# A six-layer attention stack with a selective scan: the end of the last group but one is given out behind the gates of the last feed-forward, and the ends' rows of x use the first norms' buffers

## The chip, the cores and the metric

The kernel runs on one core of a Trainium2 chip. The metric is the device time of one execution in microseconds (us), lower is better. A core has five engines with a queue each: PE (matrix products and transposes), DVE (vector work), ACT (functions by table, copies out of PSUM), POOL (general element-wise work) and SP, which only issues DMAs here. Each engine works through its own instructions in order, and semaphores join them.

## The reference

The input x has 16 sequences of 256 tokens with 128 features. It is normalised once; the normalised x goes into two branches, and the result is x plus the product of the two.

```python
xn = layernorm(x)
s = selective_scan_branch(xn)        # conv, silu, 16 states, output projection
g = silu(transformer(xn))            # 6 layers, below
return x + s * g

# transformer
for i in range(6):
    x = attn_layer(shift_tokens(x), Wqkv[i], ...) + x     # 16 heads of 64, windows of 32 with look-back
    x = ffn_layer(shift_tokens(x), ...) + x

def ffn_layer(x, g, bln, W1, b1, W2, b2):
    xn = (x - mean) / sqrt(var + 1e-05) * g + bln
    a, gate = split(xn @ W1 + b1)                         # 341 columns each
    return a * gelu(gate) @ W2 + b2
```

`shift_tokens` takes half of the features from the token before. For this case it only means that the kernel writes the two halves of the features with an offset of one token.

## The kernel before

The state x of the transformer stays in SBUF through all layers, transposed (`xT`, features by tokens). The attention works on blocks of 128 tokens: 32 blocks in a layer, 192 in all. The feed-forward works on groups of 512 tokens, two sequences, so eight groups in a layer, numbered 0 to 7. The scan branch runs beside the layers and has put its result `s_of[g]` for each group in DRAM long before the end.

The order of all instructions is written out by hand: the scheduler of the framework is off, and every engine gets its instructions in the order in which the Python code issues them. The main loop runs over n, the number of the block; each turn goes through a fixed list of steps (`order`), each of them for a block some turns ahead or behind. Three of the entries in it are `feed`. A `feed` moves the feed-forward that is at the head of the list `feeds` on to its next `yield`. One feed-forward is put on the list every four turns, as soon as the attention of its group is done.

The stages of `feed_forward` between its yields are, for a group g: the transposes out of `xT` (L336) and the copy `xt` (L340); the statistics (L162, L163, and L167 to L179 on POOL); the norm on ACT (L181); the transposes back (L189) and the copy with gain and bias (L348); the first matrix (L359), the gelu (L367) and the gates (L370); and the second matrix (L382) with the residual sum into `xT` (L385). In the last layer the last stage also puts g on the list `ending`.

`end(g)` writes one group of the result. It loads the rows of x (`xr`, L400) and the scan's result (`sT`, L402), takes the silu of the transformer's state (L405), multiplies it by `sT` (L407), transposes the product (L411), adds the rows of x (L412) and stores `out` (L413). At most one end is given out in each turn, after all steps of the turn. So the end of group g stands behind the whole last stage of the feed-forward of g, and ahead of what the next turn gives out.

The last feed-forward, that of group 7, is put on the list in the last turn, and runs alone after the loop: `feed` is called until it is done, then the last end is given out. The end of group 6 is given out at the end of the last turn, before it.

Tiles of a pool that have the same tag share buffers in turn. Three matter here:

- `xt`, one buffer: the feed-forward's `xt` and the end's `xr`.
- `gl`, two buffers: the three gelu results of a feed-forward and then `sT`.
- `first`, two buffers: the rows of x for the first norms, used only at the beginning (groups 0 to 7).

The feed-forward takes PSUM bank 7 (`f`) for L336, L189 and L382, so L336 of a group has to wait until the residual sum L385 of the group before has read the bank; the end takes bank 1 (`n`) for L411.

Of the kernel before, what the change touches and what calls it, by code (L numbers as in the profile page):

```python
# [8 lines left out]
FP = mybir.dt.float32  # L9
# [6 lines left out]
B, L, DM = 16, 256, 128  # L16
# [8 lines left out]
NG = NT // G  # L25
# [5 lines left out]
def tile_kernel(ctx: ExitStack, tc: tile.TileContext, a, out):  # L31
# [6 lines left out]
    ff = ctx.enter_context(tc.tile_pool(name="ff", bufs=1))  # L38
# [8 lines left out]
    def pair(name):  # L47
        i = int(where[name])
        return psum[:, i : i + 2, :].rearrange("p b x -> p (b x)")

    def bank(name):
        return psum[:, int(where[name]), :]
# [72 lines left out]
    def make_constants():  # L125
        nc.vector.tensor_tensor(twice, mp[:, 2:3], mp[:, 2:3], ALU.add)
        nc.vector.tensor_copy(ident_h, ident)
        nc.vector.tensor_copy(mask, mask_f)
        nc.vector.tensor_tensor(
            w_conv, taps, w_in.unsqueeze(1).to_broadcast([128, 4, 2 * DM]), ALU.mult  # L130
        )
# [7 lines left out]
    def load_ffn_weights(layer):  # L139
        w1 = wts.tile([128, 2 * DI], FP, name="w1")  # L140
        nc.sync.dma_start(out=w1, in_=a["W1"][layer])
        w2 = wts.tile([128, 3, DM], FP, name="w2")
        for c, (c0, n) in enumerate(CH):
            nc.sync.dma_start(out=w2[0:n, c, :], in_=a["W2"][layer, c0 : c0 + n, :])
        ffw_of[layer] = w1, w2
# [25 lines left out]
    def row_stats(pool, xt):  # L171
        mv = pool.tile([128, 4, 2], FP, name="mv", bufs=2)
        bn_rows(pool, mv, xt, range(4))
        return mv, row_rstd(pool, mv)

    def normed(pool, to, xt, mv, rstd):
        less = pool.tile([128, 4], FP, name="less", bufs=2)
        nc.gpsimd.tensor_tensor(less, mv[:, :, 0], rstd, ALU.mult)
        nc.gpsimd.tensor_scalar(less, less, -1.0, None, ALU.mult)  # L179
        for i in range(4):  # L180
            nc.scalar.activation(  # L181
                to[:, i, :], xt[:, i, :], AF.Identity,
                bias=less[:, i : i + 1], scale=rstd[:, i : i + 1],
            )

    def turned(xt, name):
        pt = bank(name)
        for i in range(4):
            nc.tensor.transpose(pt[:, i * 128 : (i + 1) * 128], xt[:, i, :], ident)  # L189
        return pt  # L190
# [3 lines left out]
    def first_norm(g):  # L194

        if len(first_rows) <= g:
            first_rows.append(load_first(g))
        xt = first_rows[g]
        yield
        stats = row_stats(ff, xt)  # L200
        yield
        normed(ff, xt, xt, *stats)
        yield
        pt = turned(xt, "n")
        xn_of[g] = far.tile([128, G], FP, name="xn", bufs=NG)
        for hh, o in halves:
            at = xT[hh, 2 * g : 2 * g + 2, o : o + L]
            nc.scalar.copy(at, pt[hh].rearrange("p (s t) -> p s t", s=2))
            nc.sync.dma_start(out=xn_of[g][hh].rearrange("p (s t) -> p s t", s=2), in_=at)
        yield  # L210
# [116 lines left out]
    def feed_forward(layer, g):  # L327
        if g == 0:
            load_ffn_weights(layer)
        w1, w2 = ffw_of[layer]  # L330
        yield
        yield
        pt = bank("f")
        for i in range(4):
            c0 = (i % NB) * 128
            nc.tensor.transpose(  # L336
                pt[:, i * 128 : (i + 1) * 128], xT[:, 2 * g + i // NB, c0 : c0 + 128], ident
            )
        xt = ff.tile([128, 4, DM], FP, name="xt")
        nc.scalar.copy(xt.rearrange("p n d -> p (n d)"), pt)  # L340
        stats = row_stats(ff, xt)
        yield
        normed(ff, xt, xt, *stats)
        yield
        yield
        pt = turned(xt, "f")
        xn = ff.tile([128, G], FP, name="xn")
        nc.scalar.activation(  # L348
            xn, pt, AF.Identity,
            bias=lnp[:, 1, layer : layer + 1], scale=lnp[:, 0, layer : layer + 1],  # L350
        )
        yield
        yield
        yield
        u = ff.tile([128, 3, G], FP, name="u")
        for c, (c0, n) in enumerate(CH):
            ph = pair(f"h{c}")
            for i in range(2):
                nc.tensor.matmul(  # L359
                    ph[0:n, i * G : (i + 1) * G],  # L360
                    w1[:, i * DI + c0 : i * DI + c0 + n],
                    xn,
                    start=True,
                    stop=True,
                )
            gl = ff.tile([128, G], FP, name="gl", bufs=2)
            nc.scalar.activation(  # L367
                gl[0:n], ph[0:n, G : 2 * G], AF.Gelu, bias=b1[0:n, layer, 3 + c : 4 + c]
            )
            nc.vector.scalar_tensor_tensor(  # L370
                u[0:n, c, :],
                ph[0:n, 0:G],
                b1[0:n, layer, c : c + 1],
                gl[0:n],
                ALU.add,
                ALU.mult,
            )
        yield
        yield
        po = bank("f")  # L380
        for c, (c0, n) in enumerate(CH):
            nc.tensor.matmul(po, w2[0:n, c, :], u[0:n, c, :], start=(c == 0), stop=(c == 2))  # L382
        for hh, o in halves:
            res = xT[hh, 2 * g : 2 * g + 2, o : o + L]
            nc.vector.scalar_tensor_tensor(  # L385
                res,
                po[hh].rearrange("p (s t) -> p s t", s=2),
                b2[hh, layer : layer + 1],
                res,
                ALU.add,  # L390
                ALU.add,
            )
        if layer == DEPTH - 1:
            ending.append(g)
        yield


    def end(g):
        xr = ff.tile([128, 4, DM], FP, name="xr", tag="xt")
        nc.sync.dma_start(out=xr, in_=x_rows[:, 4 * g : 4 * g + 4, :])  # L400
        sT = ff.tile([128, G], FP, name="sT", tag="gl", bufs=2)
        nc.sync.dma_start(out=sT, in_=s_of[g])  # L402
        sg = ff.tile([128, 2, L], FP, name="xn")
        for hh, o in halves:
            nc.scalar.activation(sg[hh], xT[hh, 2 * g : 2 * g + 2, o : o + L], AF.Silu)  # L405
        sg = sg.rearrange("p s t -> p (s t)")
        nc.vector.tensor_tensor(sg, sg, sT, ALU.mult)  # L407
        pt = bank("n")
        for i in range(4):
            cc = slice(i * 128, (i + 1) * 128)  # L410
            nc.tensor.transpose(pt[:, cc], sg[:, cc], ident)  # L411
        nc.vector.tensor_tensor(xr, pt.rearrange("p (n d) -> p n d", n=4), xr, ALU.add)  # L412
        nc.sync.dma_start(out=out_rows[:, 4 * g : 4 * g + 4, :], in_=xr)  # L413
# [318 lines left out]

    feeds, ending = [], []

    def clock():

# [22 lines left out]
    def feed():  # L761
        if feeds:
            try:
                next(feeds[0])
            except StopIteration:
                feeds.pop(0)
# [51 lines left out]
    last = DEPTH * BL - 1  # L818
    with tc.manual_schedule():
        norms = [first_norm(0), first_norm(1)]  # L820
        for _ in norms[0]:
            pass
        make_constants()
        make_tab(0)
        load_wqkv(0, 2)
        load_wo(0)
        for n in range(-4, last + 2):
            for g in range(2, NG):
                if n == 3 * g - 9:
                    norms.append(first_norm(g))  # L830

            layer = n // BL + 1
            if 0 < layer < DEPTH:
                if n % BL == BL // 2:
                    load_wqkv(layer, 0)
                    load_qks(layer)
                elif n % BL == BL // 2 + 4:
                    make_tab(layer)
            now[:] = next(scan, (None, None))
            for step, ahead, *args in order:  # L840

                if step in (guess, refine, close, residual) and (n + ahead) % 2 == 0:
                    continue
                if ahead is None:
                    step(*args)
                elif 0 <= n + ahead <= last:
                    step(n + ahead, *args)
            if ending:
                end(ending.pop(0))
            if n >= 4 and n % 4 == 0:  # L850
                feeds.append(feed_forward((n - 4) // BL, (n - 4) % BL // 4))
        while feeds:
            feed()
        for g in ending:
            end(g)

# [88 lines left out]
```

## Time and profile before

| | us |
|---|---|
| median of 3 runs | 3457.33 |
| lowest and highest | 3450.86, 3460.79 |
| the profiled execution | 3454.1 |
| its span in the profile | 3452.3 |

The mean clock that TensorE was granted in it is 0.987 of full speed.

The span runs from the first to the last instruction of the profile; the device time has about 2 us around it. In the lines of the profile that follow, a group of instructions is named by the line of the kernel, the engine, the operation and the tiles (result, then operands); `[4.73 <-DMA out<-xr]` says that the engine was idle for 4.73 us before it and that the landing of that transfer ended the idle time. The costliest groups of the whole run belong to the attention, which the change doesn't touch:

```profile
L480 POOL TENSOR_TENSOR t<-t,t 128x1024 f32<-128x1024 f32 x384 | 958.8, 2506 | 359.6 <-DVE den L683 210.3
L437 PE MATMUL psum<-wqkv,xT 128*128 128x512 f32 x2304 | 1067.8, 599 | 9.0 <-ACT aT L566 5.0
```

Here the columns after the bar are busy time in us, the mean of one in ns, and the idle time of the engine just before, with what ended most of it.

### The profile page before, as it was taken

The page shows a single profiled execution, that of the slowest core. Times are in us where ns is not written, and L with a number is a line of the kernel's source. Part 1 is how long each engine was busy: PE and PEld are TensorE (multiplying, and loading weights), DVE is VectorE, ACT ScalarE, POOL GpSimd, SP SyncE. Part 2 cuts the span into 40 slices and gives each one's busy share as a digit, 9 for nine tenths or more (in the row PEclk, how much of TensorE's full clock was granted, in tenths as well). Part 3 has the DMA queues.
Part 4 walks back from the last instruction along what each step waited for, and adds up shares of the span by engine and source line. Part 5 has one row for each costly group of instructions (what it writes and reads, how often), then busy time and mean ns, then how long its engine had stood idle before and what let it go on. Part 6 is the DMA issues. An engine that isn't in the chain of part 4 may idle for free.

```text
span 3452.3 us, 139990 instructions
## 1 busy us (share of the span) xinstructions
PE 3280.4 (95%) x62176; PEld 2186.9 (63%) x62176; DVE 2758.3 (80%) x3642; ACT 2135.5 (62%) x2741; POOL 2592.6 (75%) x2362
## 2 busy tenths in 40 slices
PE   7999999999999999999999999999999999999996
PEld 3666666666666666666666666666666666666664
DVE  6787878887888788878977898778979887677663
ACT  4666666665766576657655666566656666656654
POOL 6688858885888689868986798679968996555550
PEclk9999999999999999999999999999999999999998
DMA  3434333433333333333333333334323332222221
GB/s 93 109 92 107 82 81 99 103 85 82 103 94 92 90 101 96 84 85 91 108 87 88 91 99 88 86 94 100 96 76 98 98 100 70 69 62 67 69 66 56
DMA packets 191850, 305.03 MB, mean 88 GB/s; under 512 B 32719, under 2 KB 58637, under 8 KB 191245
## 3 DMA queue, kind: packets, MB, share of 16 engines
q1 hardware_dynamic: 190956, 295.74, 33.1%
q8 instruction: 489, 8.01, 1.0%
q14 instruction: 117, 0.95, 0.1%
q10 hardware_dynamic: 288, 0.33, 0.0%
HBM read 95.33 MB, written 8.91 MB: 30 GB/s over the span
## 4 chain that ended last, share of the span: by engine, by line
PE 79%; DVE 8%; ACT 5%; issue 3%; POOL 3%; DMA 0%; SPq 0%; DVEq 0%; POOLq 0%; ACTq 0%
PE psum L437 25%; PE psum L562 14%; PE psum L718 10%; PE psum L667 8%; PE psum L359 7%; PE psum L611 6%; PE psum L382 3%; ACT oT L566 3%; DVE o L691 2%; PE psum L597 2%; PE psum L231 2%; DVE hs L298 1%; DVE t L469 1%; DVE ss L514 1%; POOL t L480 1%
## 5 line engine op out<-in xcount | busy, mean ns | idle before, releaser
L480 POOL TENSOR_TENSOR t<-t,t 128x1024 f32<-128x1024 f32 x384 | 958.8, 2506 | 359.6 <-DVE den L683 210.3
L437 PE MATMUL psum<-wqkv,xT 128*128 128x512 f32 x2304 | 1067.8, 599 | 9.0 <-ACT aT L566 5.0
L552 POOL TENSOR_TENSOR t<-t,y 128x1024 f32<-128x1024 f32 x384 | 722.6, 1903 | 7.5
L437 PEld LDWEIGHTS psum<-wqkv,xT 128*128 128x128 f32 x2304 | 418.3, 192 | 391.7 <-issue 308.7
L458 DVE TENSOR_TENSOR t<-psum,tab 128x1024 f32<-128x1024 f32 x384 | 468.4, 1220 | 161.4 <-PE psum L437 150.7
L566 ACT COPY aT<-psum 128x1024 f32<-128x1024 f32 x192 | 194.3, 1012 | 563.9 <-PE psum L562 563.9
L469 DVE TENSOR_TENSOR t<-psum,tab 128x1024 f32<-128x1024 f32 x384 | 466.4, 1215 | 0.0
L514 DVE TENSOR_REDUCE ss<-sq 128x16 f32<-128x1024 f32 x384 | 456.6, 1199 | 1.3
L562 PE MATMUL psum<-ident,t 128*128 128x128 f32 x3072 | 412.6, 277 | 21.8 <-issue 9.8
L667 PEld LDWEIGHTS psum<-v,aT 64*32 64x32 f32 x24576 | 295.2, 105 | 177.2 <-issue 127.3
L448 ACT ACTIVATE sq<-psum 128x1024 f32<-128x1024 f32 x384 | 394.9, 1028 | 15.5 <-DVE t L469 10.8
L718 PE MATMUL psum<-oT,wo 128*128 128x256 f32 x1536 | 357.5, 386 | 24.2 <-ACT oT L566 24.1
L562 PEld LDWEIGHTS psum<-ident,t 128*128 128x128 f32 x3072 | 340.2, 141 | 43.4 <-issue 14.1
L667 PE MATMUL psum<-v,aT 64*32 64x65 f32 x24576 | 331.8, 227 | 26.2 <-issue 24.6
L718 PEld LDWEIGHTS psum<-oT,wo 128*128 128x128 f32 x1536 | 283.8, 190 | 81.7 <-ACT oT L566 47.0
L490 ACT COPY vt<-psum 128x1024 f32<-128x1024 f32 x192 | 196.1, 1022 | 203.6 <-PE psum L437 203.6
L611 PEld LDWEIGHTS psum<-kT,qT 64*32 64x32 f32 x24576 | 283.9, 105 | 12.1 <-issue 1.7
L611 PE MATMUL psum<-kT,qT 64*32 64x64 f32 x24576 | 287.6, 226 | 2.2 <-issue 2.2
L566 ACT COPY oT<-psum 128x1024 f32<-128x1024 f32 x192 | 195.3, 1017 | 129.8 <-PE psum L562 127.2
L298 DVE TENSOR_TENSOR_SCAN hs<-dA,bc 128x512 f32<-128x512 f32 x128 | 271.5, 2121 | 0.0
L624 DVE TENSOR_REDUCE top<-psum 128x16 f32<-128x1024 f32 x192 | 233.4, 1216 | 46.3 <-PE psum L611 46.2
L359 PE MATMUL psum<-xn,w 128*128 128x512 f32 (+1 forms) x576 | 264.0, 609 | 5.5 <-ACT o L684 4.6
(104 smaller groups left out, 4601.2 us busy)
## 6 DMA issues: line engine op xcount, KB each, us to landing
v<-vt SPq DMA_DIRECT2D x1152, 130.0 KB, 2.4
bc<-rows SPq DMA_DIRECT2D x128, 512.0 KB, 5.1
v<-vt SPq DMA_DIRECT2D x576, 65.0 KB, 2.7
wqkv<-in_Wqkv SPq DMA_DIRECT2D x18, 512.0 KB, 6.5
wo<-in_Wo SPq DMA_DIRECT2D x6, 512.0 KB, 4.2
first<-in_x SPq DMA_DIRECT2D x8, 256.0 KB, 5.0
xn<-xT SPq DMA_DIRECT2D x16, 128.0 KB, 2.7
pad<-xn SPq DMA_DIRECT2D x8, 256.0 KB
```

The costliest lines, as they stand in the source:

```text
L359: nc.tensor.matmul(ph[0:n, i * G : (i + 1) * G], w1[:, i * DI + c0 : i * DI + c0 + n], xn, start=True, stop=True,)
L437: nc.tensor.matmul(pq[:, cc], xb, wq[:, cc], start=True, stop=True)
L458: nc.vector.tensor_tensor(t1.rearrange("p (h d) -> p h d", h=H), b["pq", i].rearrange("p (h d) -> p h d", h=H), table(n, i, 0).unsqueeze(1 ...
L469: nc.vector.tensor_tensor(t2.rearrange("p (h f d) -> p h f d", h=H, f=2), b["pq", i].rearrange("p (h f d) -> p h f d", h=H, f=2)[:, :, ::- ...
L480: nc.gpsimd.tensor_tensor(b["qk", i], b["qk", i], b["t2", i], ALU.add)
L514: nc.vector.tensor_reduce(b["ss"][:, j * H : (j + 1) * H], b["sq", i].rearrange("p (h d) -> p h d", h=H), AX.X, ALU.add,)
L552: nc.gpsimd.tensor_tensor(t3, t3, b["inv"][:, j * H : (j + 1) * H].unsqueeze(2).to_broadcast([128, H, DH]), ALU.mult,)
L562: nc.tensor.transpose(pt[:, cc], of[:, cc], ident)
L566: nc.scalar.copy(to, pt.rearrange("p (c t) -> p c t", c=NP))
L611: nc.tensor.matmul(sc4[jj, r, c, :], qT[rr, c, jj], kT[rr, c, k0 : k0 + 64], start=False, stop=True, skip_group_check=True,)
L667: nc.tensor.matmul(b["pav7"][r][jj, 0:VW] if c == 7 else b["pav"][jj, r, c, :], aT[rr, c, jj], v2[rr, j, c * VW : (c + 1) * VW], start=Tru ...
L718: nc.tensor.matmul(b["pw"][:, 0:L], wo[:, c, :], b["oT"][:, c, :], start=(c == 0), stop=(c == NP - 1), skip_group_check=True,)
```

## The change

There are two parts. The rows of x for an end (`xr`) are loaded into the buffers of the tag `first`, not `xt`. And the end of group 6 isn't given out in the last turn of the loop any more, but after the loop, in the middle of the last feed-forward: behind its gates (L370) and before its second matrix (L382). A list `gated` notes which group's gates were the last to be given out. The ends of groups 0 to 5 stay where they are, and that of group 7 follows the last feed-forward as before.

```diff
@@ feed_forward, behind the gates
             )
+        gated.append(g)
         yield
         yield
         po = bank("f")
@@ end
     def end(g):
-        xr = ff.tile([128, 4, DM], FP, name="xr", tag="xt")
+        xr = ff.tile([128, 4, DM], FP, name="xr", tag="first", bufs=2)
         nc.sync.dma_start(out=xr, in_=x_rows[:, 4 * g : 4 * g + 4, :])
@@
-    feeds, ending = [], []
+    feeds, ending, gated = [], [], []
@@ the main loop and what follows it
-            if ending:
+            if ending and n <= last:
                 end(ending.pop(0))
             if n >= 4 and n % 4 == 0:
                 feeds.append(feed_forward((n - 4) // BL, (n - 4) % BL // 4))
+
         while feeds:
             feed()
+            if ending and gated[-1] == NG - 1:
+                end(ending.pop(0))
         for g in ending:
             end(g)
```

The lines of the changed kernel behind the gates have numbers that are higher by 1, and by a few more at its end; the text names them by the numbers of the kernel before.

## The prediction

> **What bounds the kernel now.** I read the engine table and the slices first, then the chain of waits for the last 85 us, then the timeline of the last 35 us, and last the stretches by granted clock. All times below are us from the start of the span.
>
> ```profile
> PE 3280.4 (95%) x62176; PEld 2186.9 (63%) x62176; DVE 2758.3 (80%) x3642; ACT 2135.5 (62%) x2741; POOL 2592.6 (75%) x2362
> PE   7999999999999999999999999999999999999996
> ```
>
> TensorE is the bound everywhere but in the first and last slice. The last slice is where the change acts, so what counts there is the serial chain and not the busy share. In the changed program PE, DVE, POOL and SP have the same number of instructions, and I compared the order on each engine with the one before: they are identical up to the last projection of the last block (L718, from 3414.29). Up to there only waits differ, and those are on transfers that landed long before. So the sum is about the last 35 us alone. The timeline of the kernel before has these pieces there:
>
> ```profile
> 3420.63 1.53 DVE L385 SCALAR_TENSOR_TENSOR xT<-psum,b,xT 64x512 f32<-64x512 f32 x2 [1.72 <-PE psum L382]
> 3424.09 0.70 PE L336 MATMUL psum<-ident,xT 128*128 128x128 f32 x4
> 3425.01 0.38 SPq L413 DMA_DIRECT2D out<-xr  x1
> 3427.55 0.58 ACT L340 COPY xt<-psum 128x512 f32<-128x512 f32 x1 [4.73 <-DMA out<-xr]
> 3435.05 6.92 PE L359 MATMUL psum<-xn,w 128*128 128x512 f32 x12 [0.87 <-ACT xn L348]
> 3442.01 0.68 ACT L367 ACTIVATE gl<-psum,b 85x512 f32<-85x512 f32 x1 [1.03 <-PE psum L359]
> 3442.71 1.28 ACT L405 ACT_TABLE_LOAD   x1
> 3444.70 1.53 DVE L385 SCALAR_TENSOR_TENSOR xT<-psum,b,xT 64x512 f32<-64x512 f32 x2 [1.22 <-PE psum L382]
> 3448.36 0.69 DVE L412 TENSOR_TENSOR xr<-psum,xr 128x512 f32<-128x512 f32 x1 [0.75 <-PE psum L411]
> ```
>
> The reader is to see that the end of group 6 stands between two parts of the last feed-forward. L385 of group 6 finishes at 3422.17; its end (L405, L407, L411, L412, the store of `out`) follows; and the copy L340 of group 7 can't start until that store has landed, because `xr` and `xt` share one buffer. The third gelu (L367) ends 3442.69, and L385 follows 2.01 later, with nothing between but the matmuls L382. The table load for the silu at 3442.71 lies beside L382.
>
> The stretches by granted clock (columns: length, busy time of PE, PEld, DVE, ACT and POOL, clock, DMA share, GB/s) give the other fact I use:
>
> ```profile
> 3366.44:3369.85 3.41, 0.00 (x0) 0.00 (x0) 0.00 (x0) 3.38 (x4) 0.00 (x0) 1.00 0.72 225
> 3376.68:3380.09 3.41, 2.25 (x18) 0.78 (x23) 1.23 (x1) 1.01 (x1) 0.00 (x0) 1.00 0.03 7
> ...
> 3421.05:3424.46 3.41, 0.86 (x8) 0.85 (x8) 1.94 (x4) 1.25 (x2) 0.00 (x0) 1.00 0.00 0
> 3424.46:3427.88 3.42, 0.33 (x3) 0.00 (x0) 0.52 (x1) 0.33 (x1) 0.00 (x0) 0.50 0.27 81
> ...
> 3431.29:3434.70 3.41, 1.64 (x4) 0.73 (x4) 0.00 (x0) 2.13 (x5) 0.52 (x3) 0.50 0.00 0
> 3434.70:3438.12 3.42, 3.06 (x4) 1.51 (x5) 0.00 (x0) 1.59 (x2) 0.00 (x0) 0.50 0.27 77
> 3438.12:3441.53 3.41, 3.41 (x9) 1.33 (x8) 1.26 (x2) 1.37 (x2) 0.00 (x0) 1.00 0.00 0
> ```
>
> Every step of the clock in the last 85 us falls on one grid of 3.41. It halves after a stretch in which PE was busy 0 or 0.86, stays full after one of 2.25, and comes back only after one of 3.06, not after 1.64.
>
> **What the Trainium skill says.** "TensorE: Matmul & The Clock Gate", section "What's actually happening", describes a free-running window of about 3413 ns that decides between full and half clock; the grid above agrees (3.41). "ScalarE: Activation LUTs", section "What ACT_TABLE_LOAD costs", gives 1283 ns plus a drain of some 1380 for a switch of sets. The trace agrees on 1.28, but shows no drain: L405's load at 2995.6 is followed by its silu at 2996.9. The measurement is used. Section "Table sets: the hidden batching unit" of the same page says that cheap functions are in every set; the changed order of ACT agrees: with the silu between them gone, the last gelus have no table load of their own any more.
>
> **The change part by part.**
>
> 1. *The `xt` buffer and the moved end: what goes.* After L385 of group 6 (3422.17) the transposes L336 of group 7 are next on PE. They wait for L385, which reads the same PSUM bank (a new wait on DVE, queued before everything else of the last feed-forward), so they can't start earlier: 0.05 for the signal, some 0.65 for four transposes, 0.05 to ACT. L340 starts at 3422.92 in place of 3427.55: gain 4.63. The wait on the store of `out` (4.73 idle on ACT) goes wholly; L336 is late next. From L340 to the end of the third gelu nothing moves: 3442.69 - 3427.55 = 15.14. The gelu's table load that vanishes is worth 0, because it lay beside L359 (ACT still waited 2.27 for PE after it). So the third gelu would end at 3438.06.
>
> 2. *The moved end: what comes in.* It is given out between the gates and L382, on all of ACT, DVE, PE and SP. On ACT, behind the third gelu: table load 1.28 and two silus 1.28, with gaps 2.60, till 3440.66. On DVE L407, 0.69, before L385: till 3441.38. On PE L411, 0.66 and 0.05 of signal, before L382: till 3442.09. So L382, which used to start beside the gates, has nothing of it done when L411 ends: six passes of 0.43, 2.58, then 0.05: L385 starts at 3444.72. Before, from the third gelu to L385 took 2.01; now 6.66. Loss 4.65. Parts 1 and 2 together: +0.02. L412 (0.69) of group 6 lies beside L382 and costs nothing.
>
> 3. *The load of `sT` for group 6* waits for the second gate, which frees a `gl` buffer, so it is issued about 1.7 before the third gate's end. The one case in which L407 waited for `sT` has it issued at 3071.58 and L407 starting at 3074.92, 3.34 later. Issue at about 3437.15 gives 3440.5, just under the 3440.66 of the silus. Taken 0; if it lands at 5.0, as `first` of the same size did, the loss is 1.5.
>
> 4. *The clock.* PE has nothing between the end of L359 and L411. L359 ends about 0.7 before the third gelu does, so the hole is 0.7 + 3.4 = 4.1, longer than a window. In before PE went straight from L359 to L382. On the grid of this trace: L359 would start at 3430.42; the window to 3431.29 holds L189 (1.64) and 0.87 of L359, which I take as not enough; the clock returns at 3434.70, so 4.28 of L359 is at half clock in place of 3.07, and all behind it moves by another 0.6: L411 at 3442.0. The window 3438.12 to 3441.53 is empty, so the clock halves at 3441.53. L411 takes 1.12 (as at 3371.62), till 3443.1; L382 has 1.84 at half clock (2.1 passes of 0.86) till 3444.94, then 3.9 passes of 0.43: it ends at 3446.6, where before it ended at 3444.65. That is +2.0. The phase of the grid is another in every execution: with no step at all the cost is 0, and with L411 and L382 wholly at half clock it is 0.46 + 2.58 = 3.0. I take +2.0.
>
> 5. *The loads of group 7.* SP puts `xr` and `sT` of group 7 behind the store of group 6, which waits for L412. Counting from the end t of that L411: L412 till t+0.72, store 0.4, `xr` 0.58, then `sT` issued at about t+1.9, landed 3.3 later at t+5.2. Its L407 would be ready at t + 2.6 + 0.1 + 1.53 + 0.65, t+4.9. So 0.3 is lost at full clock, nothing at half clock, since L382 is then longer. Before, `sT` of group 7 was issued at 3441.80, 5.1 ahead of its use.
>
> 6. *`xr` in the `first` buffers in the loop.* For groups 0 to 5 it takes a wait from L340 that had long been met, and the `first` tiles have been idle since 326 (the last L189 that reads them). Taken 0. The in-loop ends keep their cost (PE idle 5.4 before L411 in each).
>
> Sum: 0.0 + 2.0 + 0.0 = +2.0 on the profiled execution, whose device time is 3454.1 (span 3452.3); so about 3456.1 for an execution like it. The bounds are +0.3 (no step of the clock) and +4.5 (all cold, and a late `sT`). The four executions known (3450.86, 3454.1, 3457.33, 3460.79) have a mean of 3455.8 and the median shown is 3457.33; adding 2.0 gives 3457.8 and 3459.3. I take 3458.
>
> **Rivals.**
>
> A, the clock helps. If the grid lies so that it returns one window sooner in L359 (0.87 at half clock in place of 3.07, saving 1.1) and no window of the hole is empty enough, the end is 0.3 - 1.1 = -0.8: about 3456. For it: at full phase freedom it can happen; against it: a hole of 4.1 leaves hardly any position without a window under 0.86 busy.
>
> B, slower beyond the bound, by late loads. `sT` of both groups now stands on the chain, one behind a gate, one behind a store. Each us of landing above 3.3 counts twice. From a landing of 7.5 each, the loss is 2 x 4.2 + 2.0 = 10.4, 0.3% of 3457.33: 3468. Against it: with this little traffic (DMA share 0.0 to 0.3 in the tail) the longest landing of a transfer twice as large is 6.5 (`wqkv`).
>
> C, the edit only moves work: the late gate position costs what it saves and the clock does nothing, +0.3: 3456. That is parts 1 and 2 alone.
>
> That the change doesn't do what it says I exclude: the order of the instructions shows the end of group 6 behind the last gates, and `out` gone from L340's waits.
>
> **How the numbers follow.** Forecast 0.60, A 0.14, C 0.20, B 0.06. What a measurement of this kernel can tell from no change is about 0.3%, some 10.4. Forecast, A and C all lie within it. The four executions spread over 9.9, so medians of a few may differ by 4 or 5 from this alone; with that, the range is 3450 to 3466. Faster by over 0.3% would need 10.4 out of a tail in which only 4.63 can be saved: 0.05, for what I don't see outside the tail. Slower: B with some spread, 0.08. Within: 0.87.
>
> **What would show it.** L340 about 0.7 behind L385 of group 6, waiting for PE and not for a DMA; L411 of group 6 waiting some 4 on DVE; L382 of group 7 at a clock under 1.00 for part; L385 of group 7 starting some 6.7 to 9 behind the third gelu's end; L407 waiting on ACT and not on a DMA. Wrong would be: a saving kept at the end (L412 of group 7 ending clearly before 3449 on the same start), or any shift ahead of L718 of the last block.

## The result and the profile after

| | before | after |
|---|---|---|
| median of 6 executions, us | 3455.65 | 3468.26 |
| lowest and highest | 3450.86, 3460.79 | 3463.33, 3472.19 |
| profiled execution | 3454.1 | 3463.33 |
| its span | 3452.3 | 3461.5 |

The ratio is 1.0031, with an interval of 1.0017 to 1.0045. The forecast of a change within 0.3%, with 3450 to 3466 us, was wrong: the median lies above the range. The profiled execution of the changed kernel is the fastest of its six, so the two profiles are only 9.2 us apart; the other 3.4 of the 12.6 us between the medians are a matter of executions without a profile.

The timeline of the changed kernel has these pieces in the last 35 us (columns: start and duration in us, engine, line, operation; the line numbers are those of the changed kernel, so L386 is L385 of before, L406 is L405, L412 is L411, L383 is L382):

```profile
3426.34 1.51 DVE L386 SCALAR_TENSOR_TENSOR xT<-psum,b,xT 64x512 f32<-64x512 f32 x2 [1.72 <-PE psum L383]
3427.91 0.66 PE L336 MATMUL psum<-ident,xT 128*128 128x128 f32 x4 [1.61 <-DVE xT L386]
3428.61 0.59 ACT L340 COPY xt<-psum 128x512 f32<-128x512 f32 x1 [8.65 <-PE psum L336]
3436.11 8.31 PE L359 MATMUL psum<-xn,w 128*128 128x512 f32 x12 [0.87 <-ACT xn L348]
3444.46 0.68 ACT L367 ACTIVATE gl<-psum,b 85x512 f32<-85x512 f32 x1 [1.03 <-PE psum L359]
3446.45 1.27 ACT L406 ACTIVATE xn<-xT 64x512 f32<-64x512 f32 x2
3447.75 0.69 DVE L408 TENSOR_TENSOR xn<-xn,sT 128x512 f32<-128x512 f32 x1 [1.83 <-ACT xn L406]
3448.50 0.88 PE L412 MATMUL psum<-ident,xn 128*128 128x128 f32 x4 [4.08 <-DVE xn L408]
3449.17 4.25 PE L383 MATMUL psum<-u,w 128*128 128x512 f32 x6
3453.46 1.53 DVE L386 SCALAR_TENSOR_TENSOR xT<-psum,b,xT 64x512 f32<-64x512 f32 x2 [3.36 <-PE psum L383]
3457.58 0.69 DVE L413 TENSOR_TENSOR xr<-psum,xr 128x512 f32<-128x512 f32 x1 [1.20 <-PE psum L412]
```

In the kernel before, the second matrix of the same group was:

```profile
3441.81 2.84 PE L382 MATMUL psum<-u,w 128*128 128x512 f32 x6
```

The reader is to see that L340 now follows its transposes and no longer waits for a DMA; that PE waits 4.08 for the moved end; and that the second matrix takes 4.25 where it took 2.84 (a part of which was a wait for the third gate).

The stretches on the clock's grid (columns as before: length, busy times of PE, PEld, DVE, ACT, POOL, then clock, DMA share, GB/s):

```profile
3435.14:3438.55 3.41, 2.54 (x4) 1.18 (x4) 0.00 (x0) 0.78 (x1) 0.00 (x0) 0.50 0.00 0
3438.55:3441.96 3.41, 3.41 (x5) 1.35 (x4) 0.75 (x1) 0.69 (x1) 0.00 (x0) 0.50 0.00 0
3441.96:3445.38 3.42, 2.46 (x6) 0.62 (x4) 0.96 (x2) 1.59 (x3) 0.00 (x0) 1.00 0.07 7
3445.38:3448.79 3.41, 0.29 (x3) 0.30 (x4) 1.23 (x2) 2.31 (x3) 0.00 (x0) 1.00 0.25 70
3448.79:3452.20 3.41, 3.41 (x8) 1.73 (x7) 0.69 (x1) 0.00 (x0) 0.00 (x0) 0.50 0.32 83
```

A stretch with only 0.29 of PE lies in the hole, and the next one, in which most of the second matrix runs, has half the clock.

Where the time went between the two profiles, from their timelines. I cut each at the first of the sixteen products of the last projection (L718 before, L719 after), up to which the instructions are the same, and call what follows, up to the end of the last sum of rows (L412, after L413), the tail.

| piece | before | after | difference |
|---|---|---|---|
| start to the first statistic on DVE | 4.53 | 5.03 | +0.50 |
| from there to the last projection | 3409.76 | 3414.97 | +5.21 |
| the tail | 34.76 | 38.27 | +3.51 |

So 5.7 of the 9.2 us between the two profiles lie ahead of everything that the change touches. The tail by its own pieces: from the start of L385 of group 6 to L340 6.92 became 2.27 (-4.65); from there to the end of the third gelu 15.14 became 16.53 (+1.39); from there to L385 of group 7 2.01 became 8.32 (+6.31); and the rest 4.35 became 4.81 (+0.46). These four make up the 3.51.

### The profile page after: what moved, and what is told of

Same layout as the page of the kernel before. It is cut to its first block, busy times and chain, and to the rows that moved or that the text cites. A ratio compares the mean times of both kernels' runs of the same rounds, so it can differ in the third digit from the quotient of the medians.

```text
span 3461.5 us, 139986 instructions
## 1 busy us (share of the span) xinstructions
PE 3285.2 (95%) x62176; PEld 2187.6 (63%) x62176; DVE 2754.4 (80%) x3642; ACT 2134.2 (62%) x2739; POOL 2596.2 (75%) x2362
## 4 chain that ended last, share of the span: by engine, by line
PE 79%; DVE 8%; POOL 5%; ACT 4%; issue 3%; DMA 0%; SPq 0%; DVEq 0%; POOLq 0%; ACTq 0%
PE psum L438 25%; PE psum L563 14%; PE psum L719 9%; PE psum L668 8%; PE psum L359 8%; PE psum L612 6%; PE psum L383 3%; ACT oT L567 3%; DVE o L692 2%; PE psum L598 2%; PE psum L231 1%; DVE hs L298 1%; POOL t L553 1%; POOL t L481 1%; DVE t L470 1%
## 5 line engine op out<-in xcount | busy, mean ns | idle before, releaser
L668 PEld LDWEIGHTS psum<-v,aT 64*32 64x32 f32 x24576 | 294.5, 105 | 179.3 <-issue 129.3
L719 PE MATMUL psum<-oT,wo 128*128 128x256 f32 x1536 | 357.5, 386 | 24.3 <-ACT oT L567 24.3
L668 PE MATMUL psum<-v,aT 64*32 64x65 f32 x24576 | 331.6, 227 | 28.1 <-issue 26.5
L719 PEld LDWEIGHTS psum<-oT,wo 128*128 128x128 f32 x1536 | 283.8, 190 | 81.7 <-ACT oT L567 47.1
L359 PE MATMUL psum<-xn,w 128*128 128x512 f32 (+1 forms) x576 | 267.0, 615 | 4.1 <-ACT o L685 3.2
```

What stands on the lines that cost most here:

```text
L359: nc.tensor.matmul(ph[0:n, i * G : (i + 1) * G], w1[:, i * DI + c0 : i * DI + c0 + n], xn, start=True, stop=True,)
L668: nc.tensor.matmul(b["pav7"][r][jj, 0:VW] if c == 7 else b["pav"][jj, r, c, :], aT[rr, c, jj], v2[rr, j, c * VW : (c + 1) * VW], start=Tru ...
L719: nc.tensor.matmul(b["pw"][:, 0:L], wo[:, c, :], b["oT"][:, c, :], start=(c == 0), stop=(c == NP - 1), skip_group_check=True,)
```

## Experiments

Three theories: T, the change costs 2 to 5 us in the tail and the rest is the spread of executions; L, a program as loaded has a level of its own; P, the new buffer slows the part ahead of the tail. Means below are of all executions of a set; "before" is the kernel before, executed in turn with it.

### The same texts again

No edit: n1 is the kernel before, the others are the changed kernel.

> The kernel before once more, as a kernel of its own: a null comparison. Theory T (the tail: the change costs 3 to 5 us in its last 35 us, and the rest of the 12.6 us between the medians is the spread of executions that have the same instructions up to there): ratio within 0.999 to 1.001. Theory L (a program as loaded has a level of its own, through where its instructions or its tensors lie, whatever its text says): may be off by 0.1 to 0.3% though the text is the same. Theory P (the new buffer of the rows of x slows the part ahead of the tail): 1.000.

> The changed kernel once more. T: the ratio falls to about 1.001 (3 to 5 us), as the first six executions were drawn high by chance. L: anywhere from 1.000 to 1.003. P: again 1.003, and its profile has the part up to the last projection of the last block longer by some 5 to 9 us than before, with the same sign as in the first profile (there 4.6 us).

> The changed kernel a third time. T (all of the change is in the tail, 2 to 4 us; the first comparison's 1.0031 was a high draw): ratio about 1.0007, its tail from the last projection's first product to the last L412 about 38 us as in its two profiles (38.3, 38.1), the part ahead of it anywhere between 3404 and 3415. L (a program as loaded has a level of its own): this set of executions as a whole may lie 0.2% or more from the second one (3458), with little overlap.

> The changed kernel a fourth time, loaded for itself, beside a second load of it in the same call. T (the whole change is 2 to 3 us in the tail): ratio 1.0004 to 1.0010 and a tail of 36.5 to 38.5 us. L (a program as loaded has a level of its own, which the first comparison caught at 12 us above before): the two loads may differ from each other by 5 us or more in the mean, or one of them lies again at 1.003.

> The same text as the fourth, loaded once more. T: mean within 3 us of the fourth. L: apart by 5 us or more.

| set | executions | mean | mean of before (executions) | ratio, interval | tail in its profile |
|---|---|---|---|---|---|
| n1, before | 22 | 3456.6 | 3456.6 (51) | 1.0000, 0.9990 to 1.0010 | 36.9 |
| first, after | 6 | 3468.0 | 3455.6 (6) | 1.0031, 1.0017 to 1.0045 | 38.3 |
| n2, after | 14 | 3458.2 | 3456.6 (51) | 1.0007, 0.9995 to 1.0019 | 38.1 |
| n3, after | 22 | 3460.8 | 3459.5 (43) | 1.0002, 0.9992 to 1.0013 | 36.7 |
| n4, after | 22 | 3463.0 | 3457.9 (51) | 1.0018, 1.0008 to 1.0028 | 38.2 |
| n5, after | 22 | 3461.0 | 3457.9 (51) | 1.0005, 0.9996 to 1.0014 | 36.7 |

The null comparison is at 1.0000. The changed kernel lies 1.6, 1.3, 5.2 and 3.2 us above before in the four later sets, weighted by their 80 executions 2.9 us. The five tails of the changed kernel have a mean of 37.6, the two of the kernel before (34.8, 36.9) of 35.8: +1.8. That is close to the low end of what T expects. Two expectations under T missed: the tail of n3 was to be about 38 and is 36.7, and n4 was to be at 1.0004 to 1.0010 and is at 1.0018.

What the change itself makes of the tail is steadier than the tail. From L385 of group 6 to L340 it takes 2.26 or 2.27 in all five profiles of the changed kernel, against 6.92 and 7.03 in the two of before; from the third gelu to L385 of group 7 it takes 8.04 to 8.32 against 2.00. What makes the tails differ within one kernel is mostly the first matrix (L359), which falls partly at half clock: 7.50 to 8.31 in the changed kernel, 6.92 and 8.49 in that of before.

P falls: n2 has the part up to the last projection at 3403.9, shorter than in either profile of the kernel before (3409.8, 3413.7), and the three sets further down that have the new buffer without the late end (e2, e4, n6) all have means below before. L is not borne out by n4 and n5, two loads of one text 2.0 us apart. But the first set stays odd. With a spread of 5 us an execution, the difference of two means of six is uncertain by about 2.9 (5 times the root of 2/6), and 12.4 lies 3.3 times that above 2.9. Of the 80 later executions only 7 reach the first median, 3468.26. No set reproduced it, and why those six executions came out so high stays open; a part of it goes with the clock, see the last experiment.

### Each part alone

e1 has the moved end with the rows of x in the old buffer:

```diff
-        xr = ff.tile([128, 4, DM], FP, name="xr", tag="first", bufs=2)
+        xr = ff.tile([128, 4, DM], FP, name="xr", tag="xt")
```

> The end of group 6 behind the last gates, but the rows of x stay in the buffer of xt. The rows and the scan's result of group 7 are then issued only when the store of group 6 has landed, about 2.4 us later than in the changed kernel, so the last product waits about 1 us for them. T: tail about 1 us longer than in the changed kernel, total 4 to 6 us above before. P: the part ahead of the tail as before, so no more than 4 to 6 us above before, while the changed kernel is at 12. L: no order between the two.

e2 is the kernel before with the other part alone:

```diff
-        xr = ff.tile([128, 4, DM], FP, name="xr", tag="xt")
+        xr = ff.tile([128, 4, DM], FP, name="xr", tag="first", bufs=2)
```

> The rows of x in the first norms' buffers, the end of group 6 where it was before. The copy xt of the last feed-forward no longer waits for the store to land: it starts right behind its transposes, some 2.7 us sooner. T: 2 to 3 us faster than before (ratio 0.9992). P: slower than before by 5 to 9 us less 2.7. L: no order.

e1: ratio 1.0004 (0.9992 to 1.0015), tail 37.7. e2: ratio 0.9996 (0.9985 to 1.0007), mean 3454.5 against 3456.6, tail 32.8, below both tails of the kernel before. Both intervals include 1, so the parts can only be told apart in the tail. The timelines of e1 and then of e2:

```profile
3424.40 0.58 ACT L340 COPY xt<-psum 128x512 f32<-128x512 f32 x1 [8.65 <-PE psum L336]
3445.37 0.38 SPq L414 DMA_DIRECT2D out<-xr  x1
3447.68 0.37 SPq L401 DMA_DIRECT2D xr<-in_x  x1
3451.35 0.69 DVE L408 TENSOR_TENSOR xn<-xn,sT 128x512 f32<-128x512 f32 x1 [1.62 <-DMA sT<-s]
```

```profile
3427.99 1.06 PE L336 MATMUL psum<-ident,xT 128*128 128x128 f32 x4
3428.95 0.38 SPq L413 DMA_DIRECT2D out<-xr  x1
3429.09 0.58 ACT L340 COPY xt<-psum 128x512 f32<-128x512 f32 x1 [2.79 <-PE psum L336]
```

In e1 L340 waits for its transposes and not for a DMA, as in the changed kernel (2.26 behind the start of L386), though the buffer is still shared: the order alone brings the gain at L340 there. What the shared buffer costs in e1 comes later: the load of the rows is issued only 2.3 us behind the store's issue, and the product waits until `sT`, queued behind it, has landed, 1.62 in place of the 0.69 that it waits for the silus elsewhere. In e2 L340 starts while the store is still under way, 4.98 behind L385 in place of 6.92, a gain of 1.9 where 2.7 was expected. So the buffer by itself gains in the tail, and the move gives back what it gains.

### The clock in the hole

e3 keeps PE busy while it waits for the moved end, with products that nobody reads:

```diff
         gated.append(g)
+        if layer == DEPTH - 1 and g == NG - 1:
+            for _ in range(4):
+                nc.tensor.matmul(
+                    psum[:, 3, :], w1[:, 0:128], wqkv_of[layer, 2][:, 0:G], start=True, stop=True
+                )
```

> The changed kernel with four more matrix products that nobody reads, between the last first-matrix products and the transposes of the moved end: eight passes of 0.43 us, 3.4 us, which end before the product of the moved end is ready. If the empty stretch on PE halves the clock for the second matrix (step 4 of the prediction, +2), the second matrix takes 2.6 to 2.8 us again where it took 4.25, and the tail is 36 to 36.5 us in place of 38.2. If the loss is the serial chain alone, the tail stays at 38 us.

Ratio 0.9998 (0.9986 to 1.0011); tail 36.4. Its timeline:

```profile
3440.06 3.60 PE L381 MATMUL psum<-wqkv,w 128*128 128x512 f32 x8
3444.30 0.66 PE L417 MATMUL psum<-ident,xn 128*128 128x128 f32 x4 [0.65 <-DVE xn L413]
3444.80 2.74 PE L388 MATMUL psum<-u,w 128*128 128x512 f32 x6
3450.10 0.69 DVE L413 TENSOR_TENSOR xn<-xn,sT 128x512 f32<-128x512 f32 x1 [0.99 <-DMA sT<-s]
```

L388 is the second matrix: 2.74, with more work on PE, against 3.73 to 4.25 in the five profiles of the changed kernel, so the loss was the clock's and not the products'. The ratio can't show this, and the tail alone hardly (n3 and n5 have 36.7). And at full clock the last product waits for `sT` of group 7, 0.99 in all, 0.30 more than the 0.69 for which it waits for the silus elsewhere: step 5 of the prediction gave 0.3.

### A better place for the moved end

e4 and n6 give the end of group 6 out sooner, behind the statistics of the last feed-forward and ahead of its norm, and keep the buffer:

```diff
         stats = row_stats(ff, xt)
+        gated.append(g)
         yield
...
-        gated.append(g)
         yield
         yield
         po = bank("f")
```

> Both parts of the change, but the end of group 6 is given out one stage sooner: behind the statistics of the last feed-forward, where ACT, DVE and PE all wait for POOL. The gain of 4.6 us at the copy xt stays, and the table load and silus (2.6 us) lie in ACT's wait of 3.9 us, the product and transposes ahead of the transposes back. Expected: tail of 30 to 31.5 us, 4 to 5 us less than before and 7 less than in the changed kernel; ratio 0.9987. If the moved end costs wherever it stands, the tail would be 34 or more.

> The variant with the end of group 6 behind the statistics, once more. T: tail 30 to 31.5 us, ratio to before 0.999 again, and 5 to 7 us below the changed kernel of the same call.

Ratios to the kernel before: 0.9992 (0.9981 to 1.0004) and 0.9987 (0.9976 to 0.9998); means 3.2 and 5.1 us below it; tails 31.3 and 30.7. n6 has a median of 3452.12 where n4 and n5, executed in turn with it, have 3464.13 and 3461.09. The timeline of e4:

```profile
3430.94 0.59 ACT L340 COPY xt<-psum 128x512 f32<-128x512 f32 x1 [8.65 <-PE psum L336]
3431.54 1.28 ACT L406 ACT_TABLE_LOAD   x1
3432.83 1.27 ACT L406 ACTIVATE xn<-xT 64x512 f32<-64x512 f32 x2
3434.13 0.69 DVE L408 TENSOR_TENSOR xn<-xn,sT 128x512 f32<-128x512 f32 x1 [0.89 <-ACT xn L406]
3434.88 1.12 PE L412 MATMUL psum<-ident,xn 128*128 128x128 f32 x4 [3.98 <-DVE xn L408]
3435.39 1.65 ACT L181 ACTIVATE xt<-xt,less,rstd 128x128 f32<-128x128 f32 x4 [1.29 <-POOL less L179]
3446.36 2.84 PE L383 MATMUL psum<-u,w 128*128 128x512 f32 x6
```

The table load and the silus stand in the time in which ACT waits for POOL anyway: 1.29 of that wait are still left behind them, and L383 runs beside the gates again. From L340 to the third gelu, the first matrix (L360 here, L359 before) left out, it takes 8.22 in the kernel before, in e4 and in n6 alike: the end costs nothing there. Of the kernels tried this is the fastest; its second interval excludes 1, its first one doesn't. The gain in e4 (3.2 us, where 4 to 5 were expected) is not clear of the spread by itself.

### Where the spread comes from

e5 is the kernel before without the scan's 16 steps (loads of `bc`, exponentials, products, scans); y holds the direct term alone.

```diff
@@ bring
-        if n + 2 < NS:
-            bc[n + 2] = mb.tile([128, 2, G], FP, name="bc", bufs=3)
-            nc.sync.dma_start(
-                out=bc[n + 2], in_=of[g]["rows"][:, n + 2, :].partition_broadcast(128)
-            )
@@ the list of steps
-        (state, None, weigh),
...
-        (state, None, decay),
...
-        (state, None, drive),
...
-        (state, None, advance),
```

> The kernel before without the 16 steps of the scan for each group: no loads of bc, no exponentials, no products and no scan, so that y holds only the direct term and the output is not the reference's. It asks where the spread of executions comes from. In the profiles so far the part up to 2860 us, in which the scan runs, differs by 4.3 us (standard deviation), and the rest by 1.0. If the spread comes from the scan running beside the attention, the executions of this kernel spread by 1 to 2 us in place of 5. If it comes from the attention or the clock alone, they spread by 4 to 5 us as before. The time itself falls by some 1 to 4%.

Five executions lie between 3398.36 and 3401.07, a standard deviation of 1.0 (ratio 0.9833, 0.9816 to 0.9851); nine of the kernel before, in turn with them, between 3450.37 and 3467.77, a standard deviation of 5.6. So the spread comes with the scan running beside the attention. In the twelve profiles ahead of this one the times at which the same DVE instruction starts differ by a standard deviation of 4.4 at 2860 us, where the scan ends, and what is added from there to 3330 us by 1.0. By itself that shows little, since stretches of the same length while the scan runs add 0.8 to 2.7.

The granted clock says more. Between 60 and 2860 us the twelve profiles have 5 to 9 stretches of 3.41 at half clock, at places that change from one execution to the next; in the profile of e5, without the scan, there is none from 48 to 2943 us. The time at which that DVE instruction near 2860 starts goes with their number: a correlation of 0.93, and 2.7 us for each. A pass takes 0.86 at half clock and 0.43 at full, so such a stretch loses at most 1.7 us (half of 3.41), and holes on PE must count besides. PE is idle between 60 us and that instruction for 80.9 in n2 and for 90.0 in n4, the fastest and the slowest of the profiles up to there, 14.5 us apart with 5 and 9 such stretches. The wait that differs most stands before the products with the values (L668, L667 of before). First n2, then n4, from 60 to 2860 us (idle in us, times, longest):

```profile
PE psum L668 <- issue: 22.3, 20, 2.8
PE psum L668 <- issue: 29.9, 21, 3.1
```

The profile names no releaser for it, so what ends this wait stays open. Within every set but e5 and the first, executions with a lower mean clock are slower, with correlations of -0.48 to -0.89. These are correlations: a hole on PE costs time and can bring the half clock behind it, and no run took the two apart. The first set fits in: its mean clock is 0.9847, that of the 80 later executions 0.9861. At 2.8 us for each 0.001, the slope within the sets, I estimate that some 4 of the 7 us by which it lies above them go with the clock. Why its clock was low is not known.

## Why the prediction was wrong, and where it was right

**The spread, the step that failed.** The mechanism was right, and the sum of the change, +2.0, was about right. What failed is the last step, "How the numbers follow". It took the spread from four executions and wrote that "medians of a few may differ by 4 or 5 from this alone"; from that came 3450 to 3466. The medians of the first set differ by 12.6. Of this 3.5 us are in the tail of the profiles, 1.5 more than the sum; 5.7 are ahead of everything that the change touches, and 3.4 in executions without a profile. So the term that was mis-sized is the spread ahead of the tail, by e5 a matter of the scan beside the attention. Larger sets (80 executions, mean +2.9) lie within 0.3%, where the forecast was. Why six executions in a row came out so high is not settled.

**Step 1** gave 4.63 for the copy `xt`; the profiles show 4.65, with the wait that was named, L336 behind L385. By e1 this needs only the move; the buffer alone brings 1.9 there (e2). The vanished table load of the gelu cost and gained nothing, as said.

**Step 2** gave 4.65 for the end inside the gates; in e3, at full clock, the third gelu ends at 3440.94 and L391 (L385 of before) starts at 3447.58: 6.64, against 2.01 before, so 4.63. Right.

**Step 3**: L408 never waited for `sT` of group 6. Right.

**Step 4** gave 2.0 for the clock, from a hole of 4.1 on PE (4.08 in the profile): 0.6 in L359 and 1.4 behind the hole. In the first profile it was 1.39 in L359, 1.68 between gelu and residual (8.32 less the 6.64 of e3) and 0.46 at the last transposes: 3.5. What lies between gelu and residual is 1.40 to 1.68 in all five profiles, so the hole was priced right, and e3 shows its mechanism. What falls on L359 depends on the phase of the grid in one execution: over the profiles it takes 7.50 to 8.31 in the changed kernel, and n1, the kernel before, has the longest of all, 8.49. That the sum of the first profile stays within the given +0.3 to +4.5 is in part luck. On the mean of the profiles the tail is 1.8 longer, from five and two.

**Step 5**: right at full clock in mechanism and size (e3: 0.30), and hidden at half clock (the first profile, where L408 waits for ACT).

**Step 6**: no cost shows. e2, which has the new buffer alone, is at 0.9996, with the part up to the last projection at 3413.1 where the kernel before has 3409.8 and 3413.7.

**The signs.** Those named for the forecast came true: 8.32 behind the third gelu, L411 of group 6 waiting 4.08 on DVE. But of the signs of being wrong, "any shift ahead of L718 of the last block", one came true as well: 5.7 us. By n2, 5.8 shorter up to there than the kernel before, that sign can't be read from one execution: the spread alone sets it off.

**Rivals.** A would have needed a gain of the clock; no profile of the changed kernel has a tail under 36.7. B, late loads, priced at 10.4, didn't happen: L408 of group 7 waits for ACT in all five profiles of the changed kernel, and in e3, where it waits for the load, that costs 0.30. Its 3468 is the measured median by coincidence. C, no cost of the clock, is out by its mechanism, as the second matrix took 3.73 to 4.25 in every profile; by size, 0.3 against a mean of 1.8 in the tail, the executions hardly tell it from the forecast.

## What to carry to other kernels

Work that is moved to fill a hole must be placed where the engines wait for somebody else, and ahead of nothing that the chain needs: the same end of a group cost 4.6 us behind the gates, and the clock besides, and nothing behind the statistics. A buffer shared between a store and the next stage's first copy is worth a look on its own: untying it gained 1.9 us at that copy with no move at all, though the executions are too few to show it in the total. And a gain of 0.1% can't be judged from six executions that spread by 5 us: the interval of the first set, 1.0017 to 1.0045, lies wholly above those of n3 and n5, of the same kernel. Compare the stage itself in several profiles, cut at an instruction up to which both kernels are the same. What is left lies ahead of the tail: the six ends in the loop each leave PE idle for 5.4 to 6.0 us in the kernel before, and no run moved them.

## What was not expected of the hardware

The clock came back later than in the sum, though by the rule that the prediction used: the stretch from 3435.14 to 3438.55 had PE busy for 2.54 of 3.41 and was still followed by half clock, as the prediction took it for its own 2.5. The stretches of the grid in all thirteen profiles can be sorted by the busy time of PE in them and by the clock of the next one. At full clock, none with more than 1.67 us was followed by half clock, and none with less than 1.48 by full clock. At half clock, none with less than 2.62 was followed by full clock, and none with more than 3.03 by half clock. So in busy time more is needed to return than to stay. But a pass does at half clock half the work in the same time: counted in work at full speed, the return needs 1.3 to 1.5, about what staying needs. One limit on work done in a stretch would explain both; no run here was made to tell the two readings apart.

And executions of one program that spread by 17.4 us (nine of the kernel before) spread by 2.7 (five) when the scan is left out.
